# Four edits at the stage borders of a fused convolution and Laplace-layer kernel: queue of the first loads, order of the first sums, place of a small addition, split of the first combine

## Chip, cores and metric

The kernel runs on one core of one Trainium2 chip. The metric is device time in microseconds: the median over runs of one execution of the whole program. "The profile" is one execution recorded by the hardware profiler; its page and its trace give times from the start of its span.

Engines are named as the profile names them: PE is TensorE's matmul and PEld its weight load, DVE is VectorE, ACT is ScalarE, POOL is GpSimd, SP is SyncE. A "q" after an engine (SPq, ACTq) is its sequencer, which issues DMAs.

## The reference, cut to what matters

The input x has 16 images of 16 channels of 256 x 256, float32. Two layers run one after the other, each a residual on a group normalisation with 8 groups:

```
x = x + conv3x3_circular(_gn(x), weight)          # by FFT in the reference
x = x + laplace_layer(_gn(x), poles, residues)    # below
...
alpha = fft2(v)                                   # v = _gn(x)
A = 1 / (omega1 - pole1);  Bm = 1 / (omega2 - pole2)
S = einsum('ikpq,oikp,xikq->oxik', residue, A, Bm)
residue1 = einsum('biox,oxik->bkox', alpha, S)    # mixes channels i -> k at each frequency
D = einsum('biox,oikp,xikq->bikpq', alpha, A, Bm)
residue2 = einsum('bikpq,ikpq->bkpq', D, residue)
x1 = real(ifft2(residue1))
x2 = real(sum of residue2 * exp(pole1 ty) * exp(pole2 tx))
out = x1 + x2 / 256 / 256
```

## The kernel before, in words

The program is one long function, and its order of work is written by hand: each stage enters a manual schedule, so an engine executes, and a queue issues, what its part of the text says in the order of the text. Only some preparation between the stages is ordered by the tile framework. Each stage takes its SBUF buffers from pools that reuse the memory of the stage before, tile by tile: a first write to a new buffer waits until the old tile that lay there has been read, or stored, for the last time.

**Stage 1, convolution** (to about 723 us). The function conv(g) is called for 387 steps. Each step issues 16 matmuls of 32 x 32 (L238), in four row groups, which go through an image of 24 steps; ACT evicts the results to vt (L255) and sums squares (L263); DVE adds and subtracts the mirrored rows (L220, L221); SP stores the sums and differences to vD in DRAM (L281). Beside this the tables of the later stages are made, in pieces, by ACT, POOL and DVE. The loaded input rows lie in five buffers named xt, the results in four named vt.

**Stage 2, forward transform** (to about 1360 us). There are 64 units: 16 channels times four groups of four images. load_v (L645) loads a unit's rows s in four DMAs of 256 KB; the first three units' loads are issued ahead (L773), the others by SP, three units ahead. fold (L656 to L671) makes the even and odd parts: four additions, one of 512 elements, two for vq on DVE (L666, L667), one for the second half (L670), and two on POOL. lines multiplies with tables on TensorE (L678, L686), columns does the other axis (L706, L721) and puts the spectrum into spec. At the end of a channel project adds to proj, on DVE (L766) and POOL (L767), and spec goes to aD in DRAM, 4 MB; the last of these is issued by ACT (L806).

**Stage 3, mixing** (to about 2130 us). There are 32 groups of frequencies, g. weights(g) computes the pole weights: ten small DVE steps (L866 to L884) and one POOL product of 2048 elements a partition (L887) that spreads them over a masked tile w. sums(kk, w) is 16 matmuls (L909) of w with ct, a table that one DMA of 4 MB loads (L839) into memory that spec had. mix (L967) multiplies the sums sg with the spectra abd, which are cleared once by POOL (L1011) and loaded by SP (L953); the results yt are stored to yD by SP (L981). Within the loop, group g is mixed while the sums of g + 1 are made and the weights of g + 2 computed. Ahead of the loop stand, in this order: first_sums (two weight sets, 0 and 32, since group 0 needs columns from both; eight pairs of sums; a repair of two columns), the clearing and loading of abd, weights(1), and finish_projections, which adds the two halves of proj into accs (L944) and multiplies it on TensorE (L947, L948). The loop's first TensorE work is the sums of group 1.

**Stage 4, inverse transform** (to the end). There are 64 units again, k times four groups of images. combine (L1112, L1115) adds and subtracts image quarters on POOL: four tensor_tensor of 512 elements and one small tensor_scalar for four images, into u. transient_x (L1132) is a small product; along_x (L1148) and along_y (L1157, L1158) are the main matmuls, image by image; put_out (L1166 to L1171) adds v and stores the output. In a unit the next unit's v is loaded, the next u is combined and a quarter of the next channel's images is loaded by SP (L1091). The tile u has two buffers.

Of the kernel before, what the change touches and what calls it, by code (L numbers as in the profile page):

```python
# [9 lines left out]
FP = mybir.dt.float32  # L10
AF = mybir.ActivationFunctionType
ALU = mybir.AluOpType
# [4 lines left out]
B = 16  # L17
C = 16
N = 256
P = 128  # L20
# [4 lines left out]
def conv_then_laplace_kernel(ctx: ExitStack, tc: tile.TileContext, a: dict, out: bass.AP):  # L25
# [15 lines left out]
    nc = tc.nc  # L41
# [14 lines left out]
    proj = cp.tile([P, 2, B, 16, 2], FP, name="proj", tag="proj")  # L56
# [535 lines left out]
    for g in range(24 * B + 3):  # L592
# [3 lines left out]
        b, n = divmod(g, 24)  # L596
# [24 lines left out]
    def pool(stage, name, bufs=1, **kw):  # L621
        return stage.enter_context(tc.tile_pool(name=name, bufs=bufs, reuse_waits="tile", **kw))
# [17 lines left out]
    m, n = cols[:, 16:17], cols[:, 17:18]  # L640

    def load_v(i, b0, eng=nc.sync):
        s = sp.tile([P, 2, 4, N], FP, name="s", tag="s")
        for j in range(4):
            eng.dma_start(  # L645
                out=s[:, :, j], in_=vD[b0 + j][:, :, i, :].rearrange("h y x -> y h x")
            )
        return s

    def fold(i, b0, s):  # L650


        vf = f1.tile([P, 2, 2, 4, P], FP, name="vf", tag="vf")
        lo, hi = s[:, :, :, 0:P], s[:, :, :, N - 1 : P - 1 : -1]
        for j in range(4):
            nc.vector.scalar_tensor_tensor(  # L656
                vf[:, 0, 0, j], lo[:, 0, j], vmr[:, 1, b0 + j, i : i + 1], hi[:, 0, j], ALU.add, ALU.add
            )
        nc.vector.tensor_tensor(vf[:, 0, 1], lo[:, 1], hi[:, 1], ALU.add)


        vq = fp.tile([P, 2, 2, 4, 2, 64], FP, name="vq", tag="vq")

        def again(xo, eng):
            lo, hi = vf[:, xo, :, :, 0:64], vf[:, xo, :, :, P - 1 : 63 : -1]
            eng.tensor_tensor(vq[:, xo, :, :, 0], lo, hi, ALU.add)  # L666
            eng.tensor_tensor(vq[:, xo, :, :, 1], lo, hi, ALU.subtract)  # L667

        again(0, nc.vector)
        nc.vector.tensor_tensor(vf[:, 1], lo, hi, ALU.subtract)  # L670
        again(1, nc.gpsimd)  # L671
        return vq.rearrange("p e o b h x -> p e o b (h x)")
# [97 lines left out]

    units = [(i, b0) for i in range(C) for b0 in range(0, B, 4)]

    loaded = {u: load_v(*units[u], nc.scalar) for u in range(3)}  # L773
    vq = fold(*units[0], loaded.pop(0))
    nc.vector.bn_aggr(ms[:, B - 1], vst[:, B - 1])
    rest = v_stats(B - 4, B, lambda: pa.tile([P, 512], FP, name="ps_y", tag="ps_y"))
# [1 line left out]
    for u in range(len(units) + 1):  # L778
# [12 lines left out]
        if last is not None:  # L791
            i, b0 = last[:2]
# [25 lines left out]
    yp = pool(p2, "yt", 2)  # L818
# [4 lines left out]
    up = pool(p2, "uv")  # L823
# [5 lines left out]
    def new_sg(g):  # L829
        return (g0, g1)[g % 2].tile([P, N, 2 * C], FP, name="sg", tag="sg")  # L830
# [16 lines left out]
    m4, sset, fixrow = mcol[:, 0:4], mcol[:, 4:5], mcol[:, 5:6]  # L847
# [10 lines left out]
    def weights(g):  # L858

        shape = [P, 32, 4]
        u = up.tile([P, 4, 32, 4], FP, name="u", tag="u")
        w, den, e, f = (u[:, j] for j in range(4))
        pr2, pre, pim = (prU[:, j].unsqueeze(2).to_broadcast(shape) for j in range(3))
        nc.vector.tensor_tensor(  # L866
            w,
            omg[:, g].unsqueeze(1).to_broadcast(shape),
            pims.unsqueeze(2).to_broadcast(shape),
            ALU.subtract,  # L870
        )
# [12 lines left out]
        nc.vector.tensor_scalar(v[:, :, 0, 1], v[:, :, 1, 0], -1.0, None, ALU.mult)  # L884
        wt = wp.tile([P, 4, 8, 2, 32], FP, name="w", tag="w")
        full = [P, 64, 4, 8]
        nc.gpsimd.tensor_tensor(  # L887
            wt.rearrange("p a k o (i m) -> p (a k o) i m", i=4),
            v.rearrange("p a o r s -> p (a o) (r s)").unsqueeze(2).to_broadcast(full),
            m4.unsqueeze(1).unsqueeze(3).to_broadcast(full),  # L890
            ALU.mult,
        )
        return wt

    def at_once(steps):
        while True:
            try:
                next(steps)
            except StopIteration as e:
                return e.value  # L900

    def sums(kk, w):

        ps = [pg.tile([P, 2, N], FP, name="ps_s", tag="ps_s") for _ in range(2)]
        for ro in range(2):
            for iq in range(4):
                for odd in range(2):
                    rows = slice(64 * odd, 64 * odd + 64)
                    nc.tensor.matmul(  # L909
                        ps[odd][32 * iq : 32 * iq + 32, ro],  # L910
                        lhsT=w[rows, iq, kk, ro],
                        rhs=ct[rows, iq, kk],
                        start=True,
                        stop=True,
                    )
        return ps

    def first_sums():

        wt, w128 = at_once(weights(0)), at_once(weights(32))
        sg = new_sg(0)
        other = up.tile([P, 2, 2 * C], FP, name="other", tag="other")
        for kk in range(8):
            for h, w in enumerate((wt, w128)):
                fy = slice(P * h, P * h + P)
                ps = sums(kk, w)
                for odd in range(2):
                    k = slice(4 * kk + 2 * odd, 4 * kk + 2 * odd + 2)  # L930
                    copy = (nc.scalar.copy, nc.vector.tensor_copy)[odd]
                    copy(sg[:, fy, k], ps[odd][:, :, fy].rearrange("p r n -> p n r"))
                    copy(other[:, 1 - h, k], ps[odd][:, :, P * (1 - h)])
        for h in range(2):
            o, d = sg[:, P * h], other[:, h]
            nc.vector.tensor_tensor(d, d, o, ALU.subtract)
            nc.vector.scalar_tensor_tensor(o, d, fixrow, o, ALU.mult, ALU.add)
        return sg

    def finish_projections():  # L940


        accs = up.tile([P, 2, B, 16], FP, name="accs", tag="u")
        nc.vector.tensor_tensor(accs, proj[:, :, :, :, 0], proj[:, :, :, :, 1], ALU.add)  # L944
        for ro in range(2):
            ps = pm.tile([P, B, 16], FP, name="ps_o", tag="ps_mix")
            nc.tensor.matmul(ps, lhsT=jmat[:, 0], rhs=accs[:, ro], start=True, stop=False)  # L947
            nc.tensor.matmul(ps, lhsT=jmat[:, 2 - ro], rhs=accs[:, 1 - ro], start=False, stop=True)  # L948
            nc.vector.tensor_copy(o2[:, :, ro], ps)
# [56 lines left out]


    p2.enter_context(tc.manual_schedule())
    ahead = first_sums()
    for jq in range(4):  # L1010
        nc.gpsimd.memset(abd[jq], 0.0)  # L1011
        load(0, jq)
    wt = at_once(weights(1))
    finish_projections()
    unmix = None
    for g in range(32):
# [3 lines left out]
        for n in range(4):  # L1020
# [9 lines left out]
            for m in range(4):  # L1030
                o, src = mix(4 * n + m, sg, yt)
# [26 lines left out]
    up = pool(p3, "ud", 2)  # L1058
# [42 lines left out]
            )  # L1101
        return vl

    def combine(b0, yk):

        bs = slice(b0, b0 + 4)
        u = up.tile([P, 4, 4, P], FP, name="u", tag="ud")
        yr, zr, yi, zi = (yk[:, r, h, :, bs] for r in range(2) for h in range(2))
        for j, (in0, in1, o) in enumerate(
            ((zr, yr, ALU.add), (zr, yr, ALU.subtract), (zi, yi, ALU.add), (zi, yi, ALU.subtract))  # L1110
        ):
            nc.gpsimd.tensor_tensor(  # L1112
                u[:, :, j].rearrange("p b (c n) -> p c b n", c=8), in0, in1, o
            )
        nc.gpsimd.tensor_scalar(  # L1115
            u[:, :, :, 0].rearrange("p b m -> p m b"),
            yk[:, :, :, 0, bs, 0].rearrange("p r h b -> p (r h) b"),
            kap,
            None,
            ALU.mult,  # L1120
        )
        return u
# [54 lines left out]
    units = [(k, b0) for k in range(C) for b0 in range(0, B, 4)]  # L1177
    yk = y0.tile([P, 2, 2, 8, B, 16], FP, name="yk", tag="yk")
# [3 lines left out]
    vl = load_v(0, 0)  # L1182
    for b0 in range(4, B, 4):
        load_images(yk, b0, slice(0, P), nc.sync)
    u = combine(0, yk)

    def load_ahead(n):
        nonlocal y_next
# [9 lines left out]
    for n, (k, b0) in enumerate(units):  # L1198
# [176 lines left out]
```

## Time and profile before

| what | us |
|---|---|
| median of 3 runs | 2893.25 (2887.61 to 2897.32) |
| the profiled execution's own time | 2898.91 |
| its span, first to last instruction | 2897.0 |
| TensorE (PE) busy | 2667.3 |
| VectorE busy | 1940.5 |
| ScalarE busy | 1536.0 |
| GpSimd (POOL) busy | 1003.5 |
| longest POOL group: u of combine, 256 instructions | 342.2 |
| POOL product w, 33 instructions, mean of one | 3.6 |
| wait of the first sums for ct | 27.1 |
| wait of finish_projections for accs | 5.4 |

The mean granted TensorE clock of the run is 0.965 of full speed. DMA queues moved 650.63 MB; almost all went through SP's queue, 7.34 MB through ACT's and 1.97 MB through POOL's.

How to read the rows of a timeline: start and length in us, engine, line, operation, written tile <- read tiles, shape, how many instructions were merged, and in brackets how long the engine had been idle before and what ended that. A row of the chain of waits has start, length and the piece of work that the end of the program hung on. A row of windows has, for a stretch, the busy time of each engine, the granted clock, the busy share of the DMA engines and GB/s.

### The profile page before, as it was taken

How to read it: one execution, taken by the hardware profiler on the slowest of the kernel's cores; microseconds unless marked ns; L12 is line 12 of the kernel's file. 1: busy time of each engine (PE TensorE's matmuls, PEld its weight loads, DVE VectorE, ACT ScalarE, POOL GpSimd, SP SyncE). 2: the span in 40 equal slices, each digit the busy share in tenths (PEclk: the TensorE clock that was granted, in tenths of full speed). 3: DMA queues.
4: the chain of work that ended last, by engine and by line, in shares of the span. 5: the costliest groups of instructions: out<-in, count | busy, mean ns of one | idle time of the engine just before them, and what ended most of it. 6: DMA issues, size and time to landing. Idle time of an engine off the chain costs nothing.

```text
span 2897.0 us, 92787 instructions
## 1 busy us (share of the span) xinstructions
PE 2667.3 (92%) x39536; PEld 1971.8 (68%) x39536; DVE 1940.5 (67%) x3572; ACT 1536.0 (53%) x3098; POOL 1003.5 (35%) x906
## 2 busy tenths in 40 slices
PE   4878878889799999997899999999969999999998
PEld 2333334346577777775688888888868888888887
DVE  7766698886788888887444444444427666766666
ACT  3556677667466666664345555555524444444443
POOL 2232566420233333333211111111135554555553
PEclk9989998899899999998899999999989999999999
DMA  6555667665566666664466666666679999888995
GB/s 257 203 179 187 212 238 256 229 240 192 182 211 211 233 233 224 227 218 169 150 193 191 191 196 193 193 192 191 190 212 312 285 285 288 285 284 285 290 288 188
DMA packets 477335, 650.63 MB, mean 225 GB/s; under 512 B 49065, under 2 KB 458665, under 8 KB 462969
## 3 DMA queue, kind: packets, MB, share of 16 engines
q1 hardware_dynamic: 472920, 635.37, 67.0%
q8 instruction: 312, 5.11, 0.7%
q10 hardware_dynamic: 3408, 7.34, 0.7%
q0 software_dynamic: 592, 1.97, 0.3%
q14 instruction: 103, 0.84, 0.1%
HBM read 365.09 MB, written 279.45 MB: 222 GB/s over the span
## 4 chain that ended last, share of the span: by engine, by line
PE 56%; DMA 9%; DVE 6%; SPq 2%; POOL 1%; issue 1%; ACT 0%; DVEq 0%; ACTq 0%; POOLq 0%
PE ps_mix L967 15%; PE ps_s L909 8%; PE ps_y L678 8%; PE ps_y L686 8%; DMA yk<-yD 4%; PE ps_x L721 4%; PE ps_p L1148 4%; PE ps_f L1157 3%; PE ps_f L1158 3%; DMA out_y<-ol 3%; DVE r L1166 2%; PE psd L706 1%; DVE ol L1168 1%; DVE ol L1169 1%; SPq L1099 1%; DMA yD<-yt 1%
## 5 line engine op out<-in xcount | busy, mean ns | idle before, releaser
L238 PE MATMUL ps_conv<-xt,wc 32*32 32x512 f32 x12288 | 477.4, 641 | 18.0 <-ACT vt L255 11.2
L967 PEld LDWEIGHTS ps_mix<-abd,sg 128*64 128x64 f32 x8192 | 448.5, 138 | 65.5 <-ACT sg L1027 49.8
L967 PE MATMUL ps_mix<-abd,sg 128*64 128x128 f32 x8192 | 479.4, 276 | 13.4 <-ACT yt L1032 13.4
L1112 POOL TENSOR_TENSOR u<-yk 128x512 f32<-128x512 f32 x256 | 342.2, 1366 | 369.8 <-PE ps_p L1148 241.6
L694 ACT ACTIVATE t<-ps_y,vmr 128x384 f32<-128x384 f32 x512 | 297.7, 582 | 168.4 <-PE ps_y L686 157.0
L238 PEld LDWEIGHTS ps_conv<-xt,wc 32*32 32x32 f32 x12288 | 231.8, 106 | 214.8 <-issue 142.1
L1032 DVE COPY yt<-ps_mix 128x512 f32<-128x512 f32 x128 | 88.6, 692 | 363.8 <-PE ps_mix L967 231.8
L678 PE MATMUL ps_y<-tabE,vq 128*128 128x256 f32 x1024 | 313.1, 387 | 13.9 <-DVE vq L667 12.2
L887 POOL TENSOR_TENSOR w<-v,mcol 128x2048 f32<-128x2048 f32 x33 | 119.3, 3614 | 583.8 <-DVE v L884 580.8
L1157 PE MATMUL ps_f<-pt,inv 128*128 128x256 f32 x1024 | 305.8, 380 | 0.0
L686 PE MATMUL ps_y<-tabO,vq 128*128 128x256 f32 x1024 | 305.7, 380 | 0.0
L1158 PE MATMUL ps_f<-hs,ey 128*128 128x256 f32 x1024 | 305.0, 379 | 0.0
L1032 ACT COPY yt<-ps_mix 128x512 f32<-128x512 f32 x384 | 221.6, 587 | 147.2 <-PE ps_mix L967 95.8
L1148 PEld LDWEIGHTS ps_p<-inv,u 128*128 128x128 f32 x2048 | 265.1, 192 | 49.2 <-issue 24.3
L1148 PE MATMUL ps_p<-inv,u 128*128 128x128 f32 x2048 | 278.1, 279 | 12.6 <-POOL u L1115 12.5
L909 PE MATMUL ps_s<-ct,w 64*32 64x256 f32 x8448 | 260.6, 382 | 27.1 <-DMA ct<-cD 27.1
L1161 DVE TENSOR_TENSOR r<-ps_f,q 128x256 f32<-128x256 f32 x256 | 107.2, 419 | 252.1 <-ACT q L1160 252.1
L255 ACT ACTIVATE vt<-ps_conv,xq 128x512 f32<-128x512 f32 x256 | 167.1, 680 | 194.0 <-PE ps_conv L238 193.0
L1027 ACT COPY sg<-ps_s 128x512 f32<-128x512 f32 x248 | 159.9, 646 | 199.7 <-PE ps_s L909 199.5
L678 PEld LDWEIGHTS ps_y<-tabE,vq 128*128 128x128 f32 x1024 | 189.5, 190 | 90.3 <-ACT q L734 50.3
L1160 ACT COPY q<-ps_f 128x256 f32<-128x256 f32 x256 | 95.4, 373 | 290.8 <-PE ps_f L1158 290.8
L909 PEld LDWEIGHTS ps_s<-ct,w 64*32 64x32 f32 x8448 | 158.4, 107 | 92.3 <-POOL abd L1011 27.9
(214 smaller groups left out, 4165.0 us busy)
## 6 DMA issues: line engine op xcount, KB each, us to landing
xt<-in_x SPq DMA_DIRECT2D x32, 2322.0 KB, 9.6
abd<-aD SPq DMA_DIRECT2D x512, 128.0 KB, 3.3
yD<-yt SPq DMA_DIRECT2D x512, 128.0 KB, 2.6
vl<-vD SPq DMA_DIRECT2D x256, 256.0 KB, 3.9
out_y<-ol SPq DMA_DIRECT2D x128, 512.0 KB, 9.8
yk<-yD SPq DMA_DIRECT2D x63, 1024.0 KB, 8.6
s<-vD SPq DMA_DIRECT2D x244, 256.0 KB, 5.9
aD<-spec SPq DMA_DIRECT2D x15, 4096.0 KB, 13.3
```

The lines of the kernel that those rows point to most:

```text
L238: nc.tensor.matmul(acc[r][32 * c : 32 * c + 32], lhsT=ready[b][0][rows, phase, tap], rhs=halves[b][u // 2][rows, q : q + 5 : 4, 2 - tap : ...
L255: nc.scalar.activation(vt[:, r % 2], acc[r], AF.Identity, bias=ready[b][1], **by_sums)
L678: nc.tensor.matmul(ps[:, 0:N], lhsT=vf[:, xo, 0, j], rhs=tabE[:, 0 : i + 2 : i + 1], start=True, stop=False, skip_group_check=True,)
L686: nc.tensor.matmul(ps[:, P : P + N], lhsT=vf[:, xo, 1, j], rhs=tabO[:, i : C + 1 : C - i], start=False, stop=True, skip_group_check=True,)
L694: nc.scalar.activation(t[:, xo, j].rearrange("p l n -> p (l n)"), ps[:, 0:384], AF.Copy, scale=vmr[:, 0, b0 + j, i : i + 1],)
L909: nc.tensor.matmul(ps[odd][32 * iq : 32 * iq + 32, ro], lhsT=w[rows, iq, kk, ro], rhs=ct[rows, iq, kk], start=True, stop=True,)
L967: nc.tensor.matmul(ps[64 * t : 64 * t + 64, j], lhsT=sg[:, f : f + 2].rearrange("p f m -> p (f m)"), rhs=abd[jq][:, :, 2 * t + cc, 2 * jj ...
L1032: (nc.vector.tensor_copy if m == 3 else nc.scalar.copy)(o, src)
L1112: nc.gpsimd.tensor_tensor(u[:, :, j].rearrange("p b (c n) -> p c b n", c=8), in0, in1, o)
L1148: nc.tensor.matmul(ps[:, at], lhsT=u[:, n], rhs=tab, start=True, stop=True)
L1157: nc.tensor.matmul(ps[:, e], lhsT=tab, rhs=pt[:, e], start=True, stop=False)
L1158: nc.tensor.matmul(ps[:, e], lhsT=ey[:, e], rhs=hs, start=False, stop=True)
```

## The change

Four places are edited.

1. The first three units' loads of v in stage 2 are issued by POOL's queue instead of ACT's.
2. In first_sums the loop over the two weight sets is now outside and the loop over kk inside, so that all eight sums of set 0 come before those of set 32. For g = 0 alone, weights makes w in sixteen POOL products of 128 elements, in the order in which sums reads them, instead of one of 2048. Set 32 and all later groups keep the one product.
3. The addition of accs is moved from finish_projections to a place ahead of first_sums. Its tile comes from the pool of yt (tag "yt") instead of the pool of the weights' scratch (tag "u").
4. combine can do some of a unit's four images; the first unit of stage 4 calls it four times for one image each. All other units call it as before.

```
-    loaded = {u: load_v(*units[u], nc.scalar) for u in range(3)}
+    loaded = {u: load_v(*units[u], nc.gpsimd) for u in range(3)}
...
         wt = wp.tile([P, 4, 8, 2, 32], FP, name="w", tag="w")
-        full = [P, 64, 4, 8]
-        nc.gpsimd.tensor_tensor(
...
+        if g:
+            full = [P, 64, 4, 8]
+            nc.gpsimd.tensor_tensor(
...
+            return wt
+
+        full = [P, 4, 4, 8]
+        v6 = v.rearrange("p (a k) o r s -> p a k o (r s)", a=4)
+        for k in range(8):
+            for o in range(2):
+                nc.gpsimd.tensor_tensor(
+                    wt[:, :, k, o].rearrange("p a (i m) -> p a i m", i=4),
+                    v6[:, :, k, o].unsqueeze(2).to_broadcast(full),
+                    m4.unsqueeze(1).unsqueeze(3).to_broadcast(full),
+                    ALU.mult,
+                )
         return wt
...
-        for kk in range(8):
-            for h, w in enumerate((wt, w128)):
+        for h, w in enumerate((wt, w128)):
+            for kk in range(8):
...
     def finish_projections():
-        accs = up.tile([P, 2, B, 16], FP, name="accs", tag="u")
-        nc.vector.tensor_tensor(accs, proj[:, :, :, :, 0], proj[:, :, :, :, 1], ALU.add)
...
     p2.enter_context(tc.manual_schedule())
+    accs = yp.tile([P, 2, B, 16], FP, name="accs", tag="yt")
+    nc.vector.tensor_tensor(accs, proj[:, :, :, :, 0], proj[:, :, :, :, 1], ALU.add)
     ahead = first_sums()
...
-    def combine(b0, yk):
-        bs = slice(b0, b0 + 4)
-        u = up.tile([P, 4, 4, P], FP, name="u", tag="ud")
+    def combine(b0, yk, u=None, j0=0, n=4):
+        bs = slice(b0 + j0, b0 + j0 + n)
+        if u is None:
+            u = up.tile([P, 4, 4, P], FP, name="u", tag="ud")
+        us = u[:, j0 : j0 + n]
...
-                u[:, :, j].rearrange("p b (c n) -> p c b n", c=8), in0, in1, o
+                us[:, :, j].rearrange("p b (c n) -> p c b n", c=8), in0, in1, o
...
-            u[:, :, :, 0].rearrange("p b m -> p m b"),
+            us[:, :, :, 0].rearrange("p b m -> p m b"),
...
-    u = combine(0, yk)
+    u = None
+    for j in range(4):
+        u = combine(0, yk, u, j, 1)
```

More of the change, by code (lines that the diff above doesn't have):

```diff
@@ L885, in weights @@
         wt = wp.tile([P, 4, 8, 2, 32], FP, name="w", tag="w")
-        full = [P, 64, 4, 8]
[L887 to L892, printed above, removed]
+        if g:
+            full = [P, 64, 4, 8]
+            nc.gpsimd.tensor_tensor(
+                wt.rearrange("p a k o (i m) -> p (a k o) i m", i=4),
+                v.rearrange("p a o r s -> p (a o) (r s)").unsqueeze(2).to_broadcast(full),
+                m4.unsqueeze(1).unsqueeze(3).to_broadcast(full),
[9 more added lines that the diff above has]
+                    v6[:, :, k, o].unsqueeze(2).to_broadcast(full),
+                    m4.unsqueeze(1).unsqueeze(3).to_broadcast(full),
+                    ALU.mult,
+                )
         return wt
```

## The prediction, as it was put on record

> **What bounds the kernel now.** I read the page's first part, then its slices, then the chain of waits by order of time, then the timeline of each of the three borders, then the busy time by windows.
>
> ```profile
> PE 2667.3 (92%) x39536; PEld 1971.8 (68%) x39536; DVE 1940.5 (67%) x3572; ACT 1536.0 (53%) x3098; POOL 1003.5 (35%) x906
> ```
>
> TensorE is busy 92% of the span. In the windows it is busy for 580.00 of 580 us inside the mixing stage (1500 to 2080) and 316.52 of 320 in the transform stage (1040 to 1360), so nothing inside a stage can gain from a shorter wait of another engine. What the change can touch is the idle time at three borders: about 12 us near 730, 27 + 5 us near 1370 to 1406, 12 us near 2140. Border 1, from the timeline:
>
> ```profile
> 723.53 0.69 ACT L255 ACTIVATE vt<-ps_conv,xq 128x512 f32<-128x512 f32 x1 [0.41 <-PE ps_conv L238]
> 726.86 8.56 ACTq L645 DMA_DIRECT2D s<-vD  x9
> 727.58 0.35 DVE L656 SCALAR_TENSOR_TENSOR vf<-s,vmr 128x128 f32<-128x128 f32 x1
> 732.08 0.35 DVE L656 SCALAR_TENSOR_TENSOR vf<-s,vmr 128x128 f32<-128x128 f32 x1 [1.32 <-DMA s<-vD]
> 734.25 0.69 DVE L666 TENSOR_TENSOR vq<-vf 128x512 f32<-128x512 f32 x1 [1.21 <-DMA vD<-vt]
> 735.69 1.19 PE L678 MATMUL ps_y<-tabE,vq 128*128 128x256 f32 x2 [12.18 <-DVE vq L667]
> ```
>
> ACT's queue reaches the twelve loads of s only among its last evictions (first issue 724.35, nine of them after 726.86). The fold on VectorE waits for them 3.4 us in three pieces, up to 732.08. But L666 then waits once more, and not for s: vq lies on an old vt buffer whose last store must land. Border 2:
>
> ```profile
> 1366.42 3.75 POOL L887 TENSOR_TENSOR w<-v,mcol 128x2048 f32<-128x2048 f32 x1 [2.99 <-DVE u L866]
> 1371.46 0.33 SPq L839 DMA_DIRECT2D ct<-cD  x1
> 1372.75 3.60 POOL L887 TENSOR_TENSOR w<-v,mcol 128x2048 f32<-128x2048 f32 x1 [2.58 <-DVE v L884]
> 1383.93 16.95 PE L909 MATMUL ps_s<-ct,w 64*32 64x256 f32 x512 [27.07 <-DMA ct<-cD]
> 1405.77 3.89 POOL L887 TENSOR_TENSOR w<-v,mcol 128x2048 f32<-128x2048 f32 x1 [15.61 <-DVE v L884]
> 1406.25 1.22 PE L947 MATMUL ps_o<-accs,jmat 128*128 128x256 f32 x2 [5.37 <-DVE accs L944]
> 1409.96 2.70 PE L909 MATMUL ps_s<-ct,w 64*32 64x256 f32 x64
> ```
>
> Both weight sets of group 0 are finished at 1370.2 and 1376.4; the sums start at 1383.93 because ct has just landed. Later the weights of group 1 are ready at 1405.77 + 3.89 = 1409.66, and the sums of group 1 follow at 1409.96. Border 3, pieces of the chain in order of time:
>
> ```profile
> 2134.34 3.40 DMA yk<-yD
> 2137.91 4.92 POOL u L1112 x4
> 2143.34 3.78 PE ps_p L1148 x16
> ...
> 2176.61 8.93 DMA yk<-yD
> 2185.61 3.98 POOL u L1112 x2
> ```
>
> TensorE waits for all five combine instructions (to 2143.29). But 42 us later the chain comes back to a DMA: the last quarter of the second channel's images lands at 2185.54, POOL finishes u at 2190.03, and TensorE takes it at 2190.08.
>
> **What the Trainium skill says.** "TensorE: Matmul & The Clock Gate" (What's actually happening): after an idle window of some 3.4 us the array runs at half clock until a busy window has passed, and the windows run freely. The trace agrees: granted clock 0.59 in 1404 to 1408 and 0.56 in 1408 to 1412, 1.00 before and after. "DMA: Bandwidth & Descriptors" (Issuing engines are not separate DMA queues): another issuing engine gives no more bandwidth, only sequencer time. It agrees here as far as the transfers of all queues together reach 383 GB/s at most in my 2 us windows of border 1. "SBUF — State Buffer" (SBUF: two separate sides): a GpSimd instruction that reads SBUF and a VectorE one with two SBUF inputs exclude each other for a whole instruction. It agrees: L873 took 3.57 us beside the 3.75 us weight product, 0.29 at other places. The same section warns that VectorE can hold up the descriptors of POOL's own DMAs; no run here shows that.
>
> **The change part by part.**
>
> *First loads on POOL's queue.* Twelve issues leave ACT and go to POOL, which stood idle for 82.3 us before 736.89; nothing on POOL but the second half of the first fold is queued behind them. POOL's DMAs of 128 KB take 0.54 us each, the one of 960 KB 1.78; 256 KB bounded by these is 0.6 to 1.0 us, 7 to 12 us in all. They wait for the buffers of the input they overlay. From the pool sizes (6.5 KB of weights, then five xt of 18.1 KB; against 64 KB of spec, then 24 KB of s) s covers the fourth and fifth xt buffers, last used for image 14, whose convolution ends about 24 of 384 steps before the end: near 700. So s lands near 715, before 727.58, and the 3.4 us of waits go: the four L656 take 4 x 0.35, overlapped to 1.14 as in later units, L659 0.69, and L666 could start at 729.4. What is late next is the vt store. It was issued just after 728.0; the 128 of its kind take 3.8 us in the median to land, so 731.9; its 6 us in this run came from 3 MB of s in the same engines. Gain 734.25 - 732.05 = **2.2 us**; from 0 (store as slow as now) to 3.8 (2.2 us, the fastest store near there). TensorE's loop behind it keeps its 9.58 us a unit, so this stays.
>
> *Weights in sixteen pieces.* A POOL product of 128 elements (s_w, the same broadcast form) takes 0.49 us: 16 x 0.49 = 7.9 against 3.75, +4.1. accs, now first on VectorE, waits for POOL's last proj sum (to 1363.4) and takes 0.68, so weights(0) starts near 1364.1 instead of 1361.26, but its first two steps, 1.04 and 1.23 beside POOL, fall to 0.29 each: +1 us. The second set then ends near 1379 instead of 1376.4. Cover: ct, at 1383.8; cost **0**, and if ct came 5 us earlier it would be up to 2.6. The memsets and the first abd loads slip by 2 to 3 us; abd is needed at 1412.6, so they have 25 us of slack, and three loads less compete with ct: gain 0 to 0.7, I take **-0.3**.
>
> *Order set by set.* The same 512 matmuls and 64 copies: **0**, since ct releases all of it at once.
>
> *accs early.* TensorE's 5.37 us wait goes, and its eight ps_o matmuls (3.7 us at half clock) follow the sums at full clock. But the next sums still wait for weights(1), whose ten VectorE steps stand behind the last evictions as before: done at 1409.66 less some 0.3 without accs beside it. So the wait reappears behind ps_o: start at about 1409.5, **-0.5**. And now TensorE comes to it cold. Before, ps_o warmed the array from 1406.25, and only 1.6 us of sums ran at half clock (0.8 lost). Now the clock stays low for one to two windows of 3.4 us, 1.7 to 3.4 lost, middle 2.5: **+1.7**, ends +0.9 and +2.6. Border 2: -0.3 - 0.5 + 1.7 = **+0.9**.
>
> *Combine image by image.* 4 x 0.49 plus a tensor_scalar of 4 elements (0.20 to 0.36) gives image 0 after 2.2 us, at 2140.1 instead of 2143.3; all twenty instructions end near 2146.5, before the next combine can start (2146.89, when its images land). TensorE starts 3.2 us earlier and needs 2.62 us an image, POOL 2.2, so the first four units move by 3.2. Then comes 2185.5: in 2160 to 2188 the DMA share is 0.99 to 1.05, the queue is never empty, so that quarter lands when it did. What is left: POOL's last two instructions there took 3.98 us beside VectorE's sums and would take 2 x 1.27 with those 3 us earlier: u at 2188.6 instead of 2190.03. Gain **1.4 us**; ends 0 and 3.2 (the quarter lands earlier too).
>
> **Sum:** -2.2 + 0.9 - 1.4 = -2.7 us. The profiled execution took 2898.91 us (span 2897.0 and 1.9 around it), so 2896.2; it lies 5.7 above the median of the runs shown, 2893.25, which I take as base: **2890.5**.
>
> **Rivals.** (1) All three borders pay in full: 3.8 + 3.2, ct 0.7 earlier, accs 0.5, and the clock costs no more than 0.9: -7.3, 2885.9. For it: the idle times are there. Against it: L666's store, the 99% DMA share after 2160. (2) Only what lands last counts: the store still lands at 734.1, the quarter's POOL work is no faster: 0 + 0.9 + 0 = 2894.2. For it: all three waits named first by the change have a later one behind them. (3) Slower, by the loads: POOL's wait is ended not by image 14's convolution but by something of the last evictions (727). Then twelve issues of 0.8 us put the fourth at 730.2, and with 5.7 us to land (POOL's 128 KB loads) L656 ends near 736 instead of 732.4: L666 +2.5 us, and the sum is +2.5 + 0.9 - 1.4 = +2.0, 2895.2. It decides from an issue later than about 722. Against it: the sizes of the pools. (4) The first and second edit do nothing at all is part of (2).
>
> **Chances.** Forecast 0.50, rival 1 0.18, rival 2 0.18, rival 3 0.09, something outside these 0.05. A measurement of this kernel tells some 0.3% (8.7 us) from no change: 2884.6 and 2901.9. Half of rival 1's spread and a little of the rest lies below the first: faster 0.12; the tail of rival 3 and of the unknown above the second: slower 0.06; within 0.82. Range: ends of the sum -7.3 and +2.6 (0 + 2.6 + 0), with the spread of medians, 2885 to 2896.
>
> **What would show it.** Right: s loads on POOL near 700; L666 still waiting for the vt store, at about 732; L909 still released by ct; a new wait of TensorE for POOL w of some 6 us before the sums of group 1, with half clock after it; ps_p at 2140 and again a wait for POOL u near the fifth unit. Wrong: L666 right behind L659, ct landing much earlier, or the fifth unit keeping 3 us. A first matmul of the second stage later than before means rival 3.

## The result, and the profile after

| | before | after |
|---|---|---|
| median in the first comparison | 2894.41 us (4 runs) | 2898.59 us (4 runs) |
| ratio and its 95% interval | | 1.0017 [0.9999, 1.0036] |
| median in a second one, more rounds | 2893.05 us (27 runs) | 2897.40 us (22 runs) |
| ratio and its 95% interval | | 1.0017 [1.0008, 1.0026] |
| the first profiled execution | 2898.91 us, span 2897.0 | 2897.35 us, span 2895.6 |

The first comparison alone does not exclude that nothing changed; by the second, the change makes the kernel slower, by 1.7 thousandths: 4.9 us, between 2.3 and 7.5. That is less than the 0.3% the prediction named as measurable, but it has the other sign than the forecast (-2.7), and 2898.59 lies outside the stated 2885 to 2896.

The two profiled executions show the contrary (2895.6 against 2897.0), and it is worth seeing why. In the fourteen profiles of this study the convolution ends anywhere between 715.1 and 724.9 us, with the same instructions. In the two first ones it was 723.51 before and 715.49 after, 8 us in favour of after. That lies inside this scatter: kernels with the first edit and kernels without it fill the same range. So spans are of no use here; the borders are compared by **stretches** that begin at an event of their own. They come from the trace, as differences of start or end times:

- A1: from the end of the last L221 of the convolution (its last work on DVE) to L666; A2: from there to the first ps_x of the third unit, when the pipeline runs again.
- B: from the last write of spec to the first sums (the wait for ct). C1: from the first sums to the first mix; C2: to the second mix tile.
- D1: from the first ps_h of the inverse stage to the first ps_p; D2: to the ps_h of the sixth unit, after which the border is behind.

| kernel | A1 | A2 | B | C1 | C2 | D1 | D2 |
|---|---|---|---|---|---|---|---|
| before | 6.75 | 46.01 | 23.78 | 28.66 | 34.19 | 13.60 | 71.02 |
| after | 8.67 | 47.82 | 24.26 | 30.28 | 35.81 | 10.59 | 72.01 |
| after, second profile | 9.50 | 48.66 | 24.40 | 29.99 | 35.87 | 10.27 | 69.70 |

How far a stretch scatters without an edit is read from the experiments below, wherever they leave a border alone: A2 45.89 to 46.53, mean 46.11 (five kernels); B 23.57 to 24.26, mean 23.89, and C2 34.19 to 35.09, mean 34.76 (five kernels each); D2 70.57 to 71.99, mean 71.16 (nine). Against these means the change costs 1.7 and 2.6 us at A2, 0.4 and 0.5 at B, 1.1 and 1.1 at C2, and at D2 +0.8 once and -1.5 once. Sums: +4.0 and +2.7 us, both inside the measured 2.3 to 7.5.

The page's first part hardly differs; TensorE is as busy as before, and the loss is idle time and half clock at the borders:

```profile
PE 2669.0 (92%) x39536; PEld 1974.3 (68%) x39536; DVE 1936.6 (67%) x3572; ACT 1534.4 (53%) x3098; POOL 1015.5 (35%) x948
```

**Border 1** of the kernel after, from the timeline (start, length, engine, work, and in brackets the idle time before and its releaser):

```profile
715.82 5.75 POOL L645 DMA_DIRECT2D s<-vD  x8 [48.93 <-PE ps_conv L238]
718.24 0.87 SPq L281 DMA_DIRECT2D vD<-vsum  x2
719.39 1.13 DVE L656 SCALAR_TENSOR_TENSOR vf<-s,vmr 128x128 f32<-128x128 f32 x4
719.55 1.55 SPq L281 DMA_DIRECT2D vD<-vt  x2
720.44 0.69 DVE L659 TENSOR_TENSOR vf<-s 128x512 f32<-128x512 f32 x1
728.14 0.69 DVE L666 TENSOR_TENSOR vq<-vf 128x512 f32<-128x512 f32 x1 [7.02 <-issue]
729.58 1.19 PE L678 MATMUL ps_y<-tabE,vq 128*128 128x256 f32 x2 [14.09 <-DVE vq L667]
```

The four loads of unit 0 went early (issued at 663.74 to 666.17), and so the fold's three waits for s are gone: the four L656 run in one piece, as forecast. But eight loads, those of units 1 and 2, were held on POOL for 48.93 us and released only by the last matmul of the convolution. (POOL issues in order, so this shows when the buffer of unit 1 came free; that of unit 2 may have been free before.) They then go out at 715.82 to 721.57, around the last two stores of vt. And L666 does not start until 728.14. The reason "issue" means that the engine waited for nothing that the profile names; the landing times of the trace do name it: the last vt store is issued at 720.02 and lands at 727.97, 7.95 us later (6.09 before). What moves through the DMA engines in the 3 us from 721 on, while the store is under way, from the DMA view (q0 is POOL's queue, q1 is SP's with the stores; packets, MB, share of the 16 engines; packets overlap, so shares can add up to more than 100%):

```profile
q1 hardware_dynamic: 583, 0.56, 53.4%
q0 software_dynamic: 175, 0.57, 49.8%
```

In the kernel before, the 3 us from 730 on (q10 is ACT's queue):

```profile
q1 hardware_dynamic: 647, 0.63, 59.2%
q10 hardware_dynamic: 533, 0.52, 48.9%
```

In both, the stores get about half of the engines' time.

**Border 2**:

```profile
1357.20 0.69 DVE L1021 TENSOR_TENSOR accs<-proj 128x512 f32<-128x512 f32 x1 [2.06 <-POOL proj L767]
1361.27 6.09 POOL L900 TENSOR_TENSOR w<-v,mcol 128x128 f32<-128x128 f32 x16 [4.10 <-DVE u L866]
1378.20 14.69 PE L922 MATMUL ps_s<-ct,w 64*32 64x256 f32 x403 [27.55 <-DMA ct<-cD]
1396.41 0.70 PE L958 MATMUL ps_o<-accs,jmat 128*128 128x256 f32 x2
1401.36 3.60 POOL L888 TENSOR_TENSOR w<-v,mcol 128x2048 f32<-128x2048 f32 x1 [15.47 <-DVE v L884]
1405.02 3.53 PE L922 MATMUL ps_s<-ct,w 64*32 64x256 f32 x64 [6.62 <-POOL w L888]
```

ct still releases the sums; the sixteen pieces end 10.8 us ahead of that. ps_o follows the sums without the 5.37 us wait of before. Then TensorE waits 6.62 us for the weights of group 1, and the sums that follow take 3.53 us instead of 2.70: the granted clock is 0.65 from 1400 to 1404 and 0.50 from 1404 to 1408.

**Border 3**, where u is made image by image (the first rows), and 46 us later:

```profile
2134.82 1.67 POOL L1127 TENSOR_TENSOR u<-yk 128x128 f32<-128x128 f32 x4 [30.29 <-DMA yk<-yD]
2136.60 0.31 POOL L1130 TENSOR_SCALAR u<-yk,cols 128x4 f32<-128x4 f32 x1
```

```profile
2182.72 0.82 PE L1147 MATMUL ps_h<-et,o 32*32 32x256 f32 x32
2186.05 1.88 PE L1163 MATMUL ps_p<-inv,u 128*128 128x128 f32 x8 [2.51 <-POOL u L1130]
2187.72 1.06 PE L1172 MATMUL ps_f<-pt,inv 128*128 128x256 f32 x2
```

Image 0 is ready 2.09 us after its data, and the first four units run 3 us early. Then the fifth unit waits 2.51 us for the second channel's last quarter, and its first eight ps_p take 1.88 us where eight take 1.05 at full clock.

### The profile page after: what moved, and what is told of

It is laid out like the page before. It is cut to its first block, busy times and chain, and to the rows that moved or that the text cites. A ratio compares the mean times of both kernels' runs of the same rounds, so it can differ in the third digit from the quotient of the medians.

```text
span 2895.6 us, 92850 instructions
## 1 busy us (share of the span) xinstructions
PE 2669.0 (92%) x39536; PEld 1974.3 (68%) x39536; DVE 1936.6 (67%) x3572; ACT 1534.4 (53%) x3098; POOL 1015.5 (35%) x948
## 4 chain that ended last, share of the span: by engine, by line
PE 54%; DMA 10%; DVE 7%; SPq 2%; POOL 1%; issue 1%; ACT 0%; DVEq 0%; ACTq 0%; POOLq 0%
PE ps_mix L978 16%; PE ps_s L922 9%; PE ps_y L678 8%; PE ps_y L686 8%; DMA yk<-yD 6%; PE ps_x L721 4%; DMA out_y<-ol 3%; PE ps_p L1163 3%; DVE r L1181 3%; PE ps_f L1172 2%; PE ps_f L1173 2%; SPq L1112 2%; PE psd L706 1%; DVE ol L1183 1%; DVE ol L1184 1%; DVE r L1177 1%
## 5 line engine op out<-in xcount | busy, mean ns | idle before, releaser
L978 PEld LDWEIGHTS ps_mix<-abd,sg 128*64 128x64 f32 x8192 | 451.0, 138 | 63.8 <-ACT sg L1040 49.8
L1127 POOL TENSOR_TENSOR u<-yk 128x512 f32<-128x512 f32 (+1 forms) x268 | 346.4, 1322 | 369.5 <-PE ps_p L1163 249.7
```

The source lines that it names most:

```text
L978: nc.tensor.matmul(ps[64 * t : 64 * t + 64, j], lhsT=sg[:, f : f + 2].rearrange("p f m -> p (f m)"), rhs=abd[jq][:, :, 2 * t + cc, 2 * jj ...
L1127: nc.gpsimd.tensor_tensor(us[:, :, j].rearrange("p b (c n) -> p c b n", c=8), in0, in1, o)
```

## Experiments

The theory from the profile after: border 1 pays for the loads of units 1 and 2, which delay the store; border 2 for the cold clock behind a moved wait; border 3 for the same. Rivals are named with each run. The values in "measured" are the stretches defined above; ratios are to the kernel before, with the 95% interval.

### Each edit alone

Edit 1 alone:

```
-    loaded = {u: load_v(*units[u], nc.scalar) for u in range(3)}
+    loaded = {u: load_v(*units[u], nc.gpsimd) for u in range(3)}
```

> The kernel before with the first edit alone: the twelve first loads of s on POOL's queue. Read between the last L221 of the convolution and L666 (6.75 us before, 8.67 after), so that the convolution's own scatter stays out. Theory (units 1 and 2 wait for the end of the convolution on POOL and then go out among the last vt stores, so that the store which L666 waits for lands late): eight loads issued within 1 us of the last convolution matmul, the vt store some 8 us from issue to landing, L666 at 8.7 us, and 1.9 us lost. Rival (the late store was chance): L666 at 6.8 us or sooner. Forecast on record: 4.6 us. The other borders as in the kernel before.

Measured: A1 8.54, A2 47.68; eight loads issued at 719.10 to 724.13 around a convolution that ends at 718.77; the store takes 7.82 us. Ratio 1.0005 [0.9994, 1.0015]. The theory holds; the late store is no chance, and the forecast's 4.6 us is out.

Edit 2 alone (sixteen pieces, and the sets outside):

```
...
-        for kk in range(8):
-            for h, w in enumerate((wt, w128)):
+        for h, w in enumerate((wt, w128)):
+            for kk in range(8):
```

> The kernel before with the order set by set and the sixteen pieces of weights alone; accs stays where it was. Theory (both are covered by the wait for ct): from the last spec to the first sums 23.8 us and from the first sums to the first mix 28.7 us, as before, within 0.3. Rival (the pieces or the order are what makes the second border longer): from the first sums to the first mix 30.3 us, as after.

Measured: B 23.57, C1 29.25, C2 34.78. C1 is 0.25 above the bound that the theory gave, but kernels with an unedited border 2 show 28.66 to 29.56, so the bound was too tight, and no cost is seen. Ratio 0.9999 [0.9991, 1.0006].

Edit 3 alone:

```
-        accs = up.tile([P, 2, B, 16], FP, name="accs", tag="u")
-        nc.vector.tensor_tensor(accs, proj[:, :, :, :, 0], proj[:, :, :, :, 1], ALU.add)
...
     p2.enter_context(tc.manual_schedule())
+    accs = yp.tile([P, 2, B, 16], FP, name="accs", tag="yt")
+    nc.vector.tensor_tensor(accs, proj[:, :, :, :, 0], proj[:, :, :, :, 1], ALU.add)
```

> The kernel before with accs moved ahead of the first sums, alone. Theory (the wait moves behind ps_o and the sums of group 1 then run at half clock): TensorE idle some 6 to 9 us before the sums of group 1, those sums 3.5 us instead of 2.7, and from the first sums to the first mix 30.3 us instead of 28.7. Rival (accs costs nothing, or saves the 0.5 us of the forecast): 28.2 to 28.7.

Measured: TensorE idle for 6.61 us, the sums of group 1 3.89 us, C1 29.81 and C2 36.15, the longest of all kernels: 1.4 above the mean of the unedited ones. Ratio 1.0009 [0.9997, 1.0021]. The theory holds: of the second border's cost at C2, this edit makes all.

Edit 4 alone:

```
...
-    u = combine(0, yk)
+    u = None
+    for j in range(4):
+        u = combine(0, yk, u, j, 1)
```

> The kernel before with the image-by-image combine alone. From the first ps_h of the inverse stage to the first ps_p 10.6 us instead of 13.6 in every theory. Theory (what is gained comes back as a wait for the second channel's last quarter, and the cold clock that this wait leaves is paid on top): the unit that starts with that wait 15.7 us instead of 11.6, and the stretch from the first ps_h to the sixth unit's ps_h 72.0 us instead of 71.0. Rival, the forecast on record: the quarter's POOL work gets faster by 1.4 us and that stretch is 69.6 us.

Measured: D1 10.22, the fifth unit 13.11, D2 69.51. **The theory falls, and the forecast on record is right**: D2 is 1.65 below the mean of 71.16 in this profile. The wait ahead of the fifth unit was here 1.63 us, and no clock was lost. Ratio 1.0007 [0.9995, 1.0018]: the whole kernel shows no gain, and the interval ends at one of 1.4 us.

### The whole change once more

> The kernel after, unchanged, in more rounds, for two questions. First, its ratio: if the borders are what makes it slower, some 1.9 (first) + 1.5 (second) and between -1 and +1 (third) are to be had, 2.5 to 4.5 us or 1.0009 to 1.0016; if the first result was chance of the first stage, 1.0000. Second, the fifth unit of the inverse stage: the theory says that it is slow (15.7 us) only when the wait ahead of it leaves a cold clock, so at an idle time of 2 us or less it must be about 13, and ps_p to the next unit 10.7 us, as with the combine alone; a rival says that the whole change always makes it 15.7. L666 at 8.5 to 8.7 us in any case.

Measured: A1 9.50 (the store 8.79 us; longer than either theory gave), D2 69.70, the fifth unit 13.67. The same rows in this second profile of the kernel after:

```profile
2185.90 1.16 PE L1163 MATMUL ps_p<-inv,u 128*128 128x128 f32 x8 [2.17 <-POOL u L1130]
2186.90 0.60 PE L1172 MATMUL ps_f<-pt,inv 128*128 128x256 f32 x2
```

The wait was 2.17 us, 0.34 less than in the first profile, and the matmuls behind it ran at full clock. So the same kernel can fall on either side of an edge. From this ps_p to the next unit's ps_h it is 12.34 us in the first profile, and 10.67 or 10.68 here and in eleven other profiles: the cold clock costs 1.66. The windows view of the first profile and of this one for the same 4 us (after the engines' busy times come the granted clock, the DMA share and GB/s):

```profile
2184.00:2188.00 4.00, 1.95 (x9) 1.95 (x10) 0.04 (x1) 0.62 (x3) 3.90 (x5) 0.79 1.08 395
```

```profile
2184.00:2188.00 4.00, 2.10 (x14) 1.97 (x15) 0.23 (x1) 1.40 (x4) 3.90 (x5) 1.00 1.10 410
```

Where the edge lies can be read from the clock records. In all fourteen traces, between 300 and 2880 us, the granted clock changes only at points of a grid with steps of 3.413 us (to within 3 ns), and the grid lies differently in each execution. Here are the windows of that grid around the wait (TensorE's busy time comes second), first profile and then second:

```profile
2182.88:2186.29 3.41, 0.90 (x34) 0.42 (x22) 0.76 (x2) 1.57 (x5) 3.14 (x4) 1.00 1.12 384
2186.29:2189.70 3.41, 3.41 (x13) 3.05 (x13) 0.00 (x0) 0.58 (x1) 3.41 (x4) 0.50 1.00 395
```

```profile
2182.12:2185.53 3.41, 1.61 (x37) 0.74 (x35) 1.05 (x3) 1.57 (x5) 2.54 (x3) 1.00 1.07 375
2185.53:2188.95 3.42, 3.05 (x19) 2.84 (x20) 0.00 (x0) 0.66 (x2) 3.42 (x4) 1.00 1.07 414
```

In the first profile the whole wait falls into one window, in which TensorE is busy for 0.90 us, and the next window is at half clock. In the second it is cut by a grid point, its window keeps 1.61 us of work, and the clock stays. Counted over the fourteen traces from 760 to 2880 us: after each of the 72 windows at full clock with TensorE busy for less than 1.42 us came half clock; after the 8385 with more, it came once (at 1.55).

### Keeping the array warm

```
     finish_projections()
+    idle = pm.tile([P, B, 16], FP, name="ps_o", tag="ps_mix")
+    for _ in range(14):
+        nc.tensor.matmul(idle, lhsT=jmat[:, 0], rhs=accs[:, 0], start=True, stop=True)
...
+        if n == 4:
+            idle = pf.tile([P, 2, N], FP, name="ps_f", tag="ps_f")
+            for _ in range(6):
+                nc.tensor.matmul(idle[:, 0], lhsT=cosY, rhs=hs[:, 0], start=True, stop=True)
         for j in range(4):
             pt = along_x(u_now[:, j])
```

> The kernel after with idle matmuls into a PSUM tile that nobody reads: fourteen of 128x256 (0.43 us each at full clock, 6.0 us) between ps_o and the sums of group 1, and six of them (2.6 us) ahead of the first ps_p of the fifth unit. They change no wait and no data. Theory (the new waits cost half clock on top): sums of group 1 2.6 us instead of 3.5, from the first sums to the first mix 28.9 us instead of 30.3, the fifth unit 14.0 us instead of 15.7, some 2.5 to 3 us less in all. Rival (the lost time is the waits themselves, or the sums are held by something else): both stretches as in after, 30.3 and 15.7.

Measured: C1 27.99, C2 33.52, the sums of group 1 in 1.99 us up to the first mix; the fifth unit 14.39. Ratio 0.9994 [0.9985, 1.0003]. The wait for the weights stayed (sums of group 1 start 26.01 us after the first sums, against 26.82 and 26.17 in the kernel after); C2 is 2.3 us shorter than after, and 1.5 to 2.2 of that, by which of the two profiles is taken, is the clock alone. The 28.9 us of the theory for C1 are undercut. At the fifth unit ps_p starts 3.90 us after the quarter's landing, against 3.07 or 3.08 in the other kernels with the split: six idle matmuls were too many, and cost 0.8 themselves. The windows view of this kernel, whose sums of group 1 start at 1414.00:

```profile
1408.00:1412.00 4.00, 4.00 (x21) 3.51 (x20) 2.80 (x9) 0.00 (x0) 1.66 (x1) 1.00 0.00 0
1412.00:1416.00 4.00, 3.43 (x73) 2.52 (x71) 0.69 (x1) 0.66 (x1) 1.94 (x1) 1.00 0.00 0
```

Both are at 1.00, where the kernel after had 0.65 and 0.50 around the start of these sums. Against the unedited means the stretches of this profile add up to +1.4 us, while the ratio says -1.7, at most +0.9; so half a microsecond or more lies elsewhere, and was not found.

### What delays the store

Only unit 0 on POOL, the rest on SP:

```
-    loaded = {u: load_v(*units[u], nc.scalar) for u in range(3)}
+    loaded = {u: load_v(*units[u], nc.sync if u else nc.gpsimd) for u in range(3)}
```

> The kernel before with only the four loads of unit 0 on POOL's queue, and those of units 1 and 2 on SP's, where they stand behind the last vt stores. Theory (the eight loads of units 1 and 2 ahead of the store are what delays it): the vt store lands in about 4 us, L666 starts some 4.5 us after the last L221 instead of 6.75 (before) and 8.67 (after), a gain of 2.2 us on before. Rival (the store lands late by itself, as in before): L666 at 6.7 or later. A second rival: s of unit 1, now issued later, comes too late for the second fold, and the 2 us are lost again by the third unit.

Measured: A1 6.23, A2 45.48; ratio 0.9997 [0.9987, 1.0006]. Half a microsecond better than before, not 2.2. (Three kernels below have the same first border; there the store takes 4.4 to 4.7 us and A2 is 44.33 to 44.56. So the edit is worth 0.6 to 1.8 us.) SP issued unit 1's four loads ahead of the last vt stores (721.19 to 722.71, against 724.58 and 725.09 for the stores), since the buffer comes free at the convolution's end; the store took 5.53 us. So this kernel didn't do what it was made for, and the question was put again with no load of s near the store at all:

```
-    loaded = {u: load_v(*units[u], nc.scalar) for u in range(3)}
+    loaded = {0: load_v(*units[0], nc.gpsimd)}
     vq = fold(*units[0], loaded.pop(0))
+    loaded.update({u: load_v(*units[u], nc.gpsimd) for u in (1, 2)})
```

> The kernel before with unit 0's loads on POOL and those of units 1 and 2 on POOL too, but only behind POOL's half of the first fold, so that no load of s is near the last vt stores. Theory (traffic of s in the same engines is what makes the store land 5 to 8 us after its issue): the store lands in about 4 us and L666 starts some 4.6 us after the last L221, against 6.7 (before), 8.5 (twelve on POOL) and 5.3 to 6.2 (units 1 and 2 on SP); the gain is lost again, because s of unit 1 comes some 5 us late for the second fold: third unit 4 to 6 us later than before. Rival (the last store is slow by itself): L666 at 5.3 to 6.7.

```profile
721.98 0.91 SPq L281 DMA_DIRECT2D vD<-vt  x2
722.87 0.68 DVE L659 TENSOR_TENSOR vf<-s 128x512 f32<-128x512 f32 x1
725.22 0.69 DVE L666 TENSOR_TENSOR vq<-vf 128x512 f32<-128x512 f32 x1 [1.67 <-issue]
```

The store lands 2.60 us after its issue, A1 is 3.32, and the 1.67 us of idle time are all that is left of the 7.02. In the 2 us from 722 on the stores have the engines to themselves, by the DMA view:

```profile
q1 hardware_dynamic: 794, 0.76, 108.7%
```

So the traffic of s is what makes the store slow: 2.6 us with none beside it, 4.4 to 5.5 with some of it on SP, 6.0 to 6.6 with ACT's, 7.8 to 8.8 with eight loads on POOL. The rest of the theory holds too: unit 1's s is then late, A2 is 51.27, and the ratio 1.0025 [1.0015, 1.0034].

### A version that beats both

If only the late weights keep TensorE from the sums of group 1, they have to be made earlier. Set by set, the first set's w buffer is free when its eight sums are done:

```
...
+        for jq in range(4):
+            nc.gpsimd.memset(abd[jq], 0.0)
+            load(0, jq)
         for h, w in enumerate((wt, w128)):
+            if h:
+                nxt = at_once(weights(1))
             for kk in range(8):
```

> The kernel before with the sums of group 0 set by set, accs early, and the weights of group 1 worked out between the two sets (the first set's w buffer is free by then), with the clears and loads of abd ahead of them on POOL. Theory (at the second border only the late weights of group 1 keep TensorE idle once ct is there): the sums of group 1 follow ps_o without a wait and at full clock, and from the first sums to the first mix it is 17.0 + 1.7 + 2.6 us and some 0.5 for the last evictions, 22 us instead of 28.7: 6 to 7 us gained. Rival (abd is what the first mix waits for next, or VectorE with the evictions): 26 us or more.

Measured: C1 25.08, between the two; ratio 0.9982 [0.9972, 0.9991]. ps_o and the sums of group 1 follow each other at full clock (1.89 us to the first mix), abd is no bound; but TensorE waits 2.03 us for DVE's copies in the middle of the sums, and one set therefore ends later. With unit 0's loads on POOL and the others on SP in addition:

> Both of these together: unit 0's loads on POOL with units 1 and 2 on SP, and the weights of group 1 between the two sets; combine whole, as before. If the two add up: some 2 + 6.5 = 8.5 us less than the kernel before, 0.3%. If the first is lost again by the third unit: 6.5.

Measured: A2 44.56, C1 23.37; ratio 0.9979 [0.9972, 0.9987], which is 6.1 us, nearer to the 6.5 than to the 8.5. Then the ten steps of DVE were spread:

```
...
+        steps = weights(1)
         for h, w in enumerate((wt, w128)):
-            if h:
-                nxt = at_once(weights(1))
             for kk in range(8):
                 fy = slice(P * h, P * h + P)
                 ps = sums(kk, w)
+                if not h and kk in (3, 5):
+                    next(steps)
+                if not h and kk == 7:
+                    nxt = at_once(steps)
```

> The combined kernel (unit 0's loads on POOL, the others on SP; weights of group 1 between the two sets), with the three VectorE steps of those weights spread over the copies of the first set instead of standing in one block between the sets. Theory (that block held up the copies that free the banks, which is the 2.2 us wait of TensorE in the middle of the sums): first sums to first mix 21.2 us instead of 23.4, and the kernel some 9 us faster than before, 0.3%. Rival (the copies are held by POOL's product beside them): 23.4.

```profile
1373.96 18.12 PE L909 MATMUL ps_s<-ct,w 64*32 64x256 f32 x512 [27.13 <-DMA ct<-cD]
1384.92 3.60 POOL L887 TENSOR_TENSOR w<-v,mcol 128x2048 f32<-128x2048 f32 x1 [3.75 <-PE ps_s L909]
1392.01 0.70 PE L953 MATMUL ps_o<-accs,jmat 128*128 128x256 f32 x2
1393.93 1.96 PE L909 MATMUL ps_s<-ct,w 64*32 64x256 f32 x64
```

All 512 matmuls are now one block, the weights of group 1 are ready 5.4 us before their sums, and TensorE waits for nothing between the first sums and the first mix. C1 21.86 (28.66 before), C2 27.39; median 2884.57 us (19 runs) against 2892.72, ratio 0.9979 [0.9969, 0.9988]. It cannot be told from the one without the spreading by the ratio; the 1.5 us are seen in C1. Last, with the split combine and four idle matmuls ahead of the fifth unit:

> The same with the image-by-image combine and four idle matmuls (1.7 us) ahead of the fifth unit's first ps_p. Theory (with the array kept warm this edit gives what the forecast said): from the first ps_h to the sixth unit 69.5 to 70.5 us instead of 71.2, about 1 us less than the kernel without these two. Rival (what is gained at the first unit is all given back at the fifth): the same 71.2 and no gain.

Measured: D1 10.42, D2 70.85, ratio 0.9979 [0.9970, 0.9988]. Here the rival is nearer: no gain that can be seen. The quarter had landed late in this run, 57.10 us after the first ps_h. In the last two kernels the four stretches add up to 9.3 and 9.4 us less than the unedited means; the ratios say 6.1, and at most 9.0 and 8.7. Not all that the borders gain is seen in the whole, and where the rest goes was not looked for.

That landing decides D2 in nearly every run. In all kernels with the split, but for the one cold clock, D2 is the landing plus 13.7 to 14.5: 55.77 gives 69.51, 55.94 gives 69.70, 57.10 gives 70.85. Without the split it is 70.6 to 71.4 for landings from 55.1 to 57.4, bounded from the other side by the late first unit, and above that the landing counts too (58.24 gives 71.99). So in these profiles the edit is worth about 1.5 us when the quarter lands before 56, and little or nothing after 57.

## Why the prediction was wrong

**Border 1: -2.2 forecast, +1.7 to +2.6 measured. The step that failed** is "s covers the fourth and fifth xt buffers, last used for image 14", and from it "So s lands near 715", with a vt store of 3.8 us behind it. This border makes 3.9 to 4.8 of the 5.4 to 6.7 us between the forecast sum and the measured ones. The address was worked out from pool sizes for the tile s as if one lifetime held for all three buffers of s. The profile after shows two release times, neither of them near 700: four loads go out at 664, eight only at the convolution's last matmul. The three waits of the fold did go, as forecast. The forecast also had the next wait right, the vt store, and the cause of its length right ("its 6 us in this run came from 3 MB of s in the same engines"; 2.6 us with that traffic away). It then took 3.8 us for it, on the belief that the traffic was gone. With 2 MB of it squeezed into the 6 us around the store, the store took 8.

How the engines are shared is seen in the DMA views. The Trainium skill's "DMA: Bandwidth & Descriptors" (Queues, rings and completion order) says that each DMA engine takes turns between its queues packet by packet. What the profile counts as packets are not taken in equal numbers here: 583 of SP's to 175 of POOL's, which are larger (0.57 MB in 175, against 0.56 in 583). It is the time that comes out near half and half, 53.4% to 49.8%, and beside ACT's small packets too, 59.2% to 48.9%. So half the engines instead of all of them is what the stores get in either kernel. Why POOL's loads then make it 8 us and ACT's 6 is shown in part only: from 720 to 728, 1.38 MB of POOL's loads went out beside 1.03 MB of stores; from 728 to 734.2 in the kernel before, 1.17 MB of ACT's beside 1.04. The two queues together moved 302 GB/s in the one and 358 in the other, and the cause of that was not tried.

Rival 3 was this mechanism in part: it said that POOL's wait would end at the last evictions, and that a first matmul of the second stage later than before would mean it. It put its price on the wrong wait, the fold's loads, so that its +2.5 us for L666 lies near the measured +1.9 and +2.8 is luck. It is the store that pays, and from an issue as early as 716, not 722.

**Border 2: +0.9 forecast, +1.5 measured.** The kind was right in most parts: ct releases the sums, the pieces are hidden, ps_o runs at full clock, a new wait of 6.62 us ("some 6") for POOL's w, and half clock behind it. The sums of group 1 started 26.82 and 26.17 us after the first sums against 26.03, so the -0.5 for accs was not had. ct was taken at -0.3; B is 0.4 to 0.7 above the mean in all three profiles with the edits of this border together (24.26, 24.40, 24.59 in the warm run), at or above the top of the scatter, though neither edit alone shows it (23.57, 23.54). The cause of that is open. The clock term, +1.7, was net of the 0.8 us that the kernel before loses. By the warm run the loss after is 1.5 to 2.2 us; from the start of the sums of group 1 to the second mix tile it is 0.8 and 1.5 us longer than in the kernel before, inside the ends of 0.9 and 2.6 or just under. So the clock term was somewhat too large, and two terms taken as gains were none.

**Border 3: -1.4 forecast, -1.5 in one profile and +0.8 in the other, -1.65 for the edit alone.** The sum is right for a landing like that of the profile before (55.80 us after the first ps_h): ps_p 3 us earlier, all but 1.5 of it given back. The term behind it is right as well: from the landing to ps_p it is 3.07 or 3.08 us with the split, where it was 4.54. But the landing ran from 55.12 to 58.23 us in these profiles, with the split and without it, and at a late one the kernel without the split is as quick (3.10 at 57.43); that the forecast fits the edit alone so well is in part luck. What the prediction left out is that its own argument of border 2 holds here as well: the wait that comes back at the fifth unit is long enough to cool the array in some executions, at 1.66 us. The Trainium skill's "TensorE: Matmul & The Clock Gate" (What's actually happening) gives one idle window of some 3.4 us, running freely. The grid of 3.413 us agrees; that the window must be idle does not: 0.90 us of matmuls in it did not save the clock, and in all traces anything under 1.42 us of work in a window at full clock was too little. A wait of 2.51 us inside one window was therefore enough, and one of 2.17 us across a grid point was not. A wait shorter than the window is not safe, and whether it costs the clock depends on where the grid happens to lie.

The theory with which the experiments began took border 3 for a loss in every execution. Edit 4 alone and the second profile showed that it is lost in some executions only.

The rest: the borders give +2.7 to +4.0 us, the ratio 4.9 with an interval from 2.3. What lies between is inside the interval, and no stretch was found for it.

## What to carry to other kernels

When loads are moved to an idle queue, find for every buffer, not for the tile name, what last uses its memory. Loads that wait there go out in one burst when it comes free, and the burst competes with whatever store is due then; four loads that are free early are the gain, and eight that are not are the price. A wait that is moved rather than removed should be charged for the clock of the matmuls behind it, and judged by how little work it leaves in a window of 3.4 us. Ask what ends the *last* wait at a border and move that work: here making the weights of group 1 earlier, which no part of the change did, shortened the second border by 4.2 to 7.4 us (C2 against the unedited mean).

## What was not expected of the hardware

- A DMA of 256 KB occupies POOL for 0.72 us at its issue (5.75 for eight), while SP's issues of the same load took mostly 0.4 to 0.5 us.
- A product of 128 elements a partition takes POOL 0.38 us (6.09 for sixteen), less than the 0.49 of the row it was priced by (a mean that a few long ones raise: its median is 0.41); one of 2048 takes 3.60.
- The landing time of the same 256 KB store ran from 2.60 to 8.79 us, by what else was issued in the few microseconds around it.
- TensorE's clock fell after a window of the 3.413 us grid with less than 1.42 us of matmuls (72 of 72), and after one of 8385 with more; a wait of 2.51 us was enough.
- Two busy DMA queues shared the engines' time about in half (53.4 and 49.8%, 59.2 and 48.9%), with packets of 1.0 and of 3.3 KB alike.
